# Two role adapters on one core: down features dealt in runs of eight, h kept in DRAM as the image the up phase loads

## The chip, the cores and the metric

The kernel runs on one core of a Trainium2 chip. Times are microseconds on the device, from start to end of an execution. A smaller time is better. A core has five engines with queues of their own: TensorE (PE, with its weight loads as PEld), VectorE (DVE), ScalarE (ACT), GpSimd (POOL) and SyncE (SP). SP only issues transfers here; ACT issues some as well, in the same queue as its arithmetic.

## The reference

Two layers are applied one after the other to 128 samples of 128 tokens with 1024 features, all in float32. A sample has one of three roles, and the role picks the weights. Cut to what matters, one layer is:

```python
# role: one of 0..2 for each of the 128 samples; x: [128, 128, 1024]
h = einsum("bsh,bhk->bsk", x, W_down[role]) + b_down[role]      # 1024 -> 512
h = gelu(h)
u = einsum("bsk,bkh->bsh", h, W_up[role]) + b_up[role]          # 512 -> 1024
y = x + u
x = (y - mean(y)) * rsqrt(var(y) + eps) * gamma[role] + beta[role]
```

The second layer does the same to the first one's result with its own weights.

## The kernel before

The samples are sorted by role on the chip, so that 63 pairs of equal role and two left-over samples make 64 items. There are four phases: down of layer 0, up of layer 0, down of layer 1, up of layer 1. Each phase runs over all 64 items with the weights of all three roles kept in SBUF (`wall`, eight slots of three roles). A pair is multiplied in the Winograd form of a 2x2 block product: seven products s1 to s7 instead of eight, with sums of blocks made beforehand (weights: T1 to T4 on VectorE; activations: `winograd_sums`, four subtractions or additions on POOL). A product is four (down) or two (up) blocks of 128 features that are summed in a PSUM bank.

**The layout.** TensorE wants features on the partitions. A tile `xq` (down) or `hq` (up) is loaded "quartered": quarter q of the features goes to partitions 32q to 32q+31, and partition 32q+t holds the tokens t, 32+t, 64+t and 96+t for that quarter. VectorE's transpose in blocks of 32 by 32 (L525 down, L584 up) then turns this into features on partitions, tokens along the row. In the down phase, element j*32 + i of a quarter ends on partition i of block j, so partition i works with the weight rows j*32 + i, which lie 32 rows apart in DRAM. Tokens come out in their own order.

**The way of h.** A down item writes its result into a tile `h` (two buffers, tokens on partitions). `Down.finish` (L559) stores it to the DRAM tile `hd[n]` from the ACT queue, in one transfer with rows of 2 KB. An up item loads it again with `Up.load` (L573), which calls `quartered`: eight transfers from SP of 64 KB each, in pieces of 512 bytes.

**The order.** All steps stand in a heap with due times, in units of a seventh of an item; they are emitted in the order of these times, and this is the order in which each engine's queue runs. Those of an item n that matter here, with 0 as the start of its first product: load of x at -11.9 (down) or of h at -11.5 (up); the rest of an up item's load, x for the residual, at -7 (L578); `prepare` with the transposes and POOL's sums at -8.8 (down) or -5.5 (up); products at 0, 2, ..., 12; the store of h at 12.5; in an up item the normalisation from 10.4 on and the store of its result from 13.5 (L651, to `mid` after layer 0 and to the output after layer 1). Since items start 7 units apart, two items' products alternate on TensorE, and the transposes of item n+2 stand in VectorE's queue ahead of the sums that end item n.

In a down pair, s1 and s3 and s5 and s7 add into one PSUM bank "b", s4 and s6 into a bank "e", s2 goes to a bank "a". Between two of them the bank's content is read: `begin` (L547, ACT) copies it to `h`, `end` (L551, VectorE) adds it to `h` and then L552 (ACT) applies gelu, `whole` (L555) applies gelu to the bank itself. So s3 waits for L547 after s1, and s7 waits for L551 after s5. L547 of item n+2 also waits until the store of `h` of item n has landed, as there are two buffers. In an up item the same places are L603 and L608 (VectorE, adding into the residual `x`).

**The weights.** The first down weights come straight into `wall` (`load_rows`, L147), four transfers of 256 KB for each half and role: role 0 at the start from ACT and SP, roles 1 and 2 later from SP. The weights of the three later phases are loaded one role at a time during the first phase (`Sums.load`, L203, four transfers of 512 KB), their blocks and sums are stored to DRAM (L212), and they come into `wall` slot by slot around each change of phase (L724). Before its first product TensorE works through a fixed row of products of zeros (L272).

Of the kernel before, what the change touches and what calls it, by code (L numbers as in the profile page):

```python
# [10 lines left out]
F32 = mybir.dt.float32  # L11
# [8 lines left out]
P = 128  # L20
SQ = 32
NQ = P // SQ
# [4 lines left out]
def kernel(  # L27
# [23 lines left out]

    nc = tc.nc
    B, S, H = x.shape
    R, _, K = layers[0][0].shape
# [11 lines left out]
    dram = ctx.enter_context(tc.tile_pool(name="mid", bufs=1, space=bass.MemoryType.DRAM))  # L68

    NI = NPAIR + 1  # L70
    hd = [dram.tile([2, S, K], F32, tag=f"hd{n}", name=f"hd{n}") for n in range(NI)]
    mid = [dram.tile([2, S, H], F32, tag=f"mid{n}", name=f"mid{n}") for n in range(NI)]
    scratch = {
        (layer, up): {
# [7 lines left out]
    def flat(tag, bufs, name, size=2048):  # L82
        return work.tile([P, size], F32, tag=tag, name=name, bufs=bufs)
# [5 lines left out]
    class Block:  # L89


        def __init__(self, slot):
            self.slot = slot
            self.v = wall[:, slot].rearrange("p (r n) -> p r n", n=W)
# [28 lines left out]
    def bias_table(v, which):  # L123

        n = v.shape[1] // 2
        t, load = table(v, which)

        def subtract(places=slice(0, R)):
            right, left = t[:, places, n:], t[:, places, 0:n]
            nc.vector.tensor_tensor(right, right, left, ALU.subtract)  # L130

        return t, load, subtract


    rows_of = [
        wall[:, 2 * k : 2 * k + 2]
        .rearrange("p k n -> p (k n)")
        .rearrange("p (r j h c) -> p r j h c", r=R, h=2, c=K // 2)
        for k in range(2)
    ]  # L140

    def load_rows(k, place, engine, kind):
        w = layers[0][0]
        role = reg(role_of, place, [kind], R - 1)
        for q in range(NQ):
            src = w[ds(role, 1), ds(q * H // NQ + k * P, P), :]
            engine.dma_start(  # L147
                rows_of[k][ts(q, SQ), place].rearrange("p j h c -> p j (h c)"),
                src.rearrange("o (j i) c -> i (o j) c", i=SQ),
            )  # L150

    first_weights = {
# [22 lines left out]
    class Sums:  # L175
# [2 lines left out]

        def __init__(self, layer, up, k):
            self.w = layers[layer][2 if up else 0]  # L180
            self.k = k
            n = self.w.shape[2] // 2
            room = tables[:, 0:2].rearrange("p t n -> p (t n)")
            self.whole = room[:, 0 : 4 * W].rearrange("p (m c) -> p m c", c=2 * n)
            block = lambda t: t.rearrange("p (j c) -> p j c", c=n)
            quarter = room[:, 0 : 4 * W].rearrange("p (k j h c) -> p k h j c", k=2, h=2, c=n)
            self.at = {
                "B11": quarter[:, 0, 0],
                "B12": quarter[:, 0, 1],
                "B21": quarter[:, 1, 0],  # L190
                "B22": quarter[:, 1, 1],
                "T1": block(room[:, 4 * W : 5 * W]),
                "T2": block(room[:, 5 * W : 6 * W]),
            }
            self.at["T3"], self.at["T4"] = self.at["B12"], self.at["B21"]
            self.to = {name: block(t[:, k]) for name, t in scratch[layer, up].items()}

        def load(self):
            role = reg(role_of, self.k, [ENG.SP], R - 1)
            rows = self.w.shape[1] // NQ  # L200
            for q in range(NQ):
                src = self.w[ds(role, 1), ds(q * rows, rows), :]
                nc.sync.dma_start(  # L203
                    self.whole[ts(q, SQ)], src.rearrange("o (m i) c -> i (o m) c", i=SQ)
                )

        def sum(self, name):
            a, b = {"T1": ("B12", "B11"), "T2": ("B22", "T1"), "T3": ("B22", "B12"), "T4": ("B21", "T2")}[name]
# [5 lines left out]
    class Phase:  # L214
# [4 lines left out]
        def load_bias(self, which):  # L219
            self.next_bias, load, self.subtract = bias_table(self.vectors[0], which)  # L220
            load()
# [108 lines left out]
    def gathered(name, values, where):  # L330

        ps = bank_a(name + "_ps")
        n = where.shape[1]
        nc.tensor.matmul(ps[0:SQ, 0:n], values, where, start=True, stop=True)
        t = const.tile([1, n], I32, name=name)
        nc.vector.tensor_copy(t, ps[0:1, 0:n])
        return t
# [17 lines left out]
    place = gathered("place", wide_place, onehot)  # L355
# [4 lines left out]
    def reg(t, s, engines, top):  # L360
        return nc.values_load(
            t[0:1, s : s + 1],
            engines=engines,
            min_val=0,
            max_val=top,
            skip_runtime_bounds_check_because="computed on the chip, always in this range",
        )

    def set_places(item, engines):

        n = item.n
        if n < NFIRST:
            item.places = [0, 0]
        elif n < NPAIR:
            item.places = [reg(place, 2 * n, engines, R - 1)] * 2
        else:
            item.places = [reg(place, 2 * n + s, engines, R - 1) for s in range(2)]
# [5 lines left out]
    def quartered(t, srcs):  # L383

        for s, src in enumerate(srcs):
            n = src.shape[-1] // NQ
            for q in range(NQ):
                nc.sync.dma_start(
                    t[s][ts(q, SQ)], src[:, ts(q, n)].rearrange("(a t) c -> t a c", t=SQ)
                )  # L390
# [6 lines left out]
    def winograd_sums(dst, a):  # L397


        half = a.shape[2] // 2  # L400
        a11, a12, a21, a22 = (a[:, i, ts(k, half)] for i in range(2) for k in range(2))
        nc.gpsimd.tensor_tensor(dst[:, 1], a11, a21, ALU.subtract)  # L402
        nc.gpsimd.tensor_tensor(a21, a21, a22, ALU.add)
        nc.gpsimd.tensor_tensor(dst[:, 0], a21, a11, ALU.subtract)  # L404
        nc.gpsimd.tensor_tensor(dst[:, 2], a12, dst[:, 0], ALU.subtract)
# [98 lines left out]
    class Down:  # L504
# [17 lines left out]
        def prepare(self):  # L522
            self.a = flat("t", 3, "xT" + self.tag).rearrange("p (s j c) -> p s j c", s=2, c=P)
            for s in range(2):
                nc.vector.transpose(  # L525
                    self.a[:, s].rearrange("p j (a t) -> p j a t", t=SQ),
                    self.xq[s].rearrange("p a (j i) -> p j a i", i=SQ),
                )
            self.sums = None
            if self.n < NPAIR:  # L530
                self.sums = flat("s", 3, "S" + self.tag, 1792)[:, 0:1536].rearrange(
                    "p (m j c) -> p m j c", m=3, c=P
                )
                winograd_sums(self.sums, self.a)
            set_places(self, [ENG.PE, ENG.Activation])
# [20 lines left out]

        def finish(self):
            at = 12.5
            return [(at, lambda: nc.scalar.dma_start(hd[self.n].rearrange("s p n -> p s n"), self.h))]  # L559

    class Up:
        LOAD, REST, PREPARE, SEED = -11.5, -7, -5.5, -4
# [4 lines left out]
            self.tag = f"u{layer}_{n}"  # L567

        def load(self):
            self.hq = flat("q", 4, "hq" + self.tag, H).rearrange(  # L570
                "p (s a c) -> p s a c", s=2, a=NQ
            )
            quartered([self.hq[:, s] for s in range(2)], [hd[self.n][s] for s in range(2)])  # L573

        def load_rest(self):
            self.x = flat("t", 3, "x" + self.tag).rearrange("p (s n) -> p s n", s=2)
# [93 lines left out]
    for k, ph in enumerate(phases):  # L670
        for m, n in enumerate(sequence):
            base = SLOTS * (k * NI + m)
            box = {}
            kind = Up if ph.up else Down

            def load(box=box, ph=ph, n=n, kind=kind, m=m):
                item = box["item"] = kind(ph, n)
                item.early = ph is phases[0] and m == 0
                if ph is phases[2] and m == 0:
                    item.SEED = -0.6  # L680
                if m == left_over_at + 1:
                    item.SEED = -1.5
                item.load()

            at(base + kind.LOAD, load)
            at(base + kind.REST, lambda box=box: box["item"].load_rest())

            def go(box=box, base=base):
                item = box["item"]
                item.prepare()  # L690
                for time, step in item.products() + item.finish():
                    at(base + time, step)


            prepare = {1: 3.5 - base, 2: 8.6 - base}.get(m, kind.PREPARE) if k == 0 else kind.PREPARE
            at(base + (-7.2 if ph is phases[2] and m < 3 else prepare), go)
# [43 lines left out]
    ph.bias, load_bias, subtract = bias_table(ph.vectors[0], 2)  # L740
    at(-12, lambda: load_bias([0]))
    at(-12, lambda: load_rows(0, 0, nc.scalar, ENG.Activation))
    at(-10, lambda: subtract(slice(0, 1)))
    at(-11, lambda: load_rows(1, 0, nc.sync, ENG.SP))
# [52 lines left out]
```

## Time and profile before

| | us |
|---|---|
| median of three runs | 3194.6 |
| lowest and highest run | 3193.32, 3203.36 |
| profiled execution | 3197.36 |
| its span, first to last instruction | 3195.3 |

Busy shares in stretches of 100 us of that execution (the stretches are named by their start):

| from, us | what runs | PE | DVE | ACT | POOL | DMA share |
|---|---|---|---|---|---|---|
| 100 | down, layer 0 | 95.9% | 42.0% | 25.2% | 46.8% | 0.74 |
| 800 | change to up, layer 0 | 94.7% | 54.3% | 37.3% | 46.2% | 0.82 |
| 1000 | up, layer 0 | 99.1% | 77.5% | 49.9% | 72.0% | 0.69 |
| 1600 | change to down, layer 1 | 90.8% | 46.2% | 33.9% | 56.7% | 0.89 |
| 1900 | down, layer 1 | 100.0% | 29.2% | 28.1% | 37.6% | 0.48 |

How to read it: a row of a group of instructions gives line, engine, operation, the tiles it writes and reads, the count, then the busy time, the mean in ns, and the idle time of the engine before these instructions with what ended it. A row of a timeline gives start and length in us, and in brackets the idle time before it and what ended that. A row of waits gives who waited for whom: total us, number of times, longest. A row of a DMA issue gives count, KB each, and the median time from issue to landing. "SPq" and "ACTq" are the queues that issue transfers. The clock that TensorE was granted was 0.994 of full speed over the span.

### The profile page before, as it was taken

What the parts mean: (1) busy time and instruction counts of PE and PEld (TensorE: products, weight loads), DVE (VectorE), ACT (ScalarE), POOL (GpSimd) and SP (SyncE); (2) the same over time, 40 slices, a digit from 0 to 9 for tenths busy, and PEclk for the clock granted to TensorE, in tenths of its full rate; (3) what the DMA queues carried; (4) which work ended last, traced back from release to release, by engine and by line L of the source; (5) the groups of instructions that cost most, each with busy time, mean ns of one, the idle gap of its engine ahead of it and who ended that gap; (6) DMA issues with size and microseconds to landing.
All of it is one profiled execution on the core that took longest, in us unless ns stands there. A gap on an engine that the chain in (4) does not pass through costs nothing. (4 is left out here: it accounts for less than half of the span.)

```text
span 3195.3 us, 43864 instructions
## 1 busy us (share of the span) xinstructions
PE 3131.9 (98%) x10824; PEld 2054.7 (64%) x10824; DVE 1772.8 (55%) x2783; ACT 1200.4 (38%) x2824; POOL 1791.7 (56%) x1399
## 2 busy tenths in 40 slices
PE   9999999999999999999989999999999999999997
PEld 6888888888534444444468888888884444444443
DVE  3533333334477777777743323233226777778877
ACT  1222222222345454545432222222224555454554
POOL 3544444444467776777754343443435777677775
PEclk9999999999999999999999999999999999999999
DMA  6776777777787666767796444544458766666664
GB/s 162 214 209 202 209 205 207 209 207 218 248 255 221 215 213 209 219 215 214 222 268 174 128 134 127 146 135 129 134 178 292 243 213 221 220 208 224 212 223 165
DMA packets 445506, 642.88 MB, mean 201 GB/s; under 512 B 46417, under 2 KB 316242, under 8 KB 445266
## 3 DMA queue, kind: packets, MB, share of 16 engines
q1 hardware_dynamic: 405986, 560.12, 59.6%
q10 hardware_dynamic: 39280, 79.96, 6.9%
q8 instruction: 102, 1.67, 0.2%
q14 instruction: 138, 1.13, 0.1%
HBM read 405.54 MB, written 234.36 MB: 200 GB/s over the span
## 5 line engine op out<-in xcount | busy, mean ns | idle before, releaser
L411 PE MATMUL bu<-wall,hTu 128*128 (+1 forms) x2048 | 929.9, 596 | 22.1 <-DVE xu L603 14.2
L411 PEld LDWEIGHTS bu<-wall,hTu 128*128 128x128 f32 x2048 | 386.3, 191 | 522.8 <-issue 426.2
L402 POOL TENSOR_TENSOR Sd<-xTd 128x512 f32<-128x512 f32 x126 | 168.6, 1338 | 842.0 <-DVE xTd L525 827.3
L632 POOL TENSOR_TENSOR varu<-varu,mhalf 128x1 f32<-128x1 f32 x256 | 334.8, 1308 | 414.6 <-ACT varu L631 367.0
L525 DVE STREAM_TRANSPOSE xTd<-xqd 128x1024 f32<-128x1024 f32 x256 | 307.9, 1230 | 438.8 <-PE bd L411 230.7
L411 PE MATMUL bd<-wall,xTd 128*128 (+1 forms) x2080 | 491.7, 380 | 7.8 <-DVE hd L551 5.2
L635 DVE SCALAR_TENSOR_TENSOR ou<-xu,meanu,tables 128x1024 f32<-128x1024 f32 x256 | 328.8, 1284 | 302.7 <-ACT ou L630 300.5
L411 PE MATMUL eu<-wall,hTu 128*128 (+1 forms) x1040 | 490.1, 594 | 4.1 <-DMA wall<-B 3.8
L411 PE MATMUL bd<-wall,Sd 128*128 (+1 forms) x2016 | 478.0, 380 | 4.4 <-ACT hd L547 4.4
L411 PEld LDWEIGHTS bd<-wall,xTd 128*128 128x128 f32 x2080 | 394.8, 190 | 66.2 <-DVE hd L551 7.3
L411 PEld LDWEIGHTS bd<-wall,Sd 128*128 128x128 f32 x2016 | 383.6, 190 | 59.4 <-POOL Sd L404 3.3
L411 PEld LDWEIGHTS eu<-wall,hTu 128*128 128x128 f32 x1040 | 198.0, 191 | 253.9 <-issue 240.6
L552 ACT ACTIVATE hd<-hd 128x256 f32<-128x256 f32 x382 | 157.2, 416 | 490.0 <-DVE hd L551 489.7
L626 ACT ACTIVATE partu<-statu 128x2 f32<-128x2 f32 x256 | 52.1, 203 | 759.4 <-DVE xu L608 759.4
L643 POOL TENSOR_TENSOR ou<-ou,tables 128x1024 f32<-128x1024 f32 x128 | 301.3, 2354 | 1.2 <-DMA hqu<-hd 0.9
L630 ACT ACTIVATE ou<-xu,meanu 128x1024 f32<-128x1024 f32 x256 | 294.0, 1148 | 19.1 <-DMA mid<-ou 4.2
L411 PE MATMUL ed<-wall,xTd 128*128 (+1 forms) x1072 | 252.9, 379 | 0.0
L402 POOL TENSOR_TENSOR hTu<-hTu 128x256 f32<-128x256 f32 x126 | 204.3, 1621 | 79.5 <-DVE hTu L584 77.7
L411 PE MATMUL ed<-wall,Sd 128*128 (+1 forms) x1008 | 238.1, 379 | 0.0
L411 PE MATMUL ad<-wall,xTd 128*128 (+1 forms) x1008 | 238.1, 379 | 0.0
L411 PE MATMUL au<-wall,hTu 128*128 (+1 forms) x504 | 236.8, 592 | 0.0
L411 PEld LDWEIGHTS ed<-wall,xTd 128*128 128x128 f32 x1072 | 203.7, 190 | 28.1 <-ACT ou L630 0.2
(96 smaller groups left out, 3348.6 us busy)
## 6 DMA issues: line engine op xcount, KB each, us to landing
xqd<-in_x_dram SPq DMA_DIRECT2D x512, 128.0 KB, 3.0
hd<-hd ACTq DMA_DIRECT2D x128, 512.0 KB, 2.8
hqu<-hd SPq DMA_DIRECT2D x1024, 64.0 KB, 4.1
xu<-in_x_dram SPq DMA_DIRECT2D x128, 512.0 KB, 5.3
mid<-ou SPq DMA_DIRECT2D x128, 512.0 KB, 5.2
xqd<-mid SPq DMA_DIRECT2D x512, 128.0 KB, 3.5
xu<-mid SPq DMA_DIRECT2D x128, 512.0 KB, 5.8
out_dram<-ou SPq DMA_DIRECT2D x128, 512.0 KB, 4.9
```

Source lines behind the costliest of these rows:

```text
L402: nc.gpsimd.tensor_tensor(dst[:, 1], a11, a21, ALU.subtract)
L411: nc.tensor.matmul(ps[:, 0:cols], a[:, j], w.rhs(r, j, cols), start=start and j == 0, stop=j == n - 1, skip_group_check=True,)
L525: nc.vector.transpose(self.a[:, s].rearrange("p j (a t) -> p j a t", t=SQ), self.xq[s].rearrange("p a (j i) -> p j a i", i=SQ),)
L552: nc.scalar.activation(y, y, AF.Gelu)
L626: nc.scalar.mul(part, self.stat[:, s], -1.0 / H)
L630: nc.scalar.activation(box["o"], self.x[:, s], AF.Square, bias=m, accum_out=v)
L632: nc.gpsimd.tensor_tensor(v, v, mhalf[:, 0:1], ALU.pow)
L635: nc.vector.scalar_tensor_tensor(box["o"], self.x[:, s], box["m"][:, 0:1], row(self.ph.gamma), ALU.add, ALU.mult)
L643: nc.gpsimd.tensor_tensor(o, o, row(self.ph.beta), ALU.add)
```

## The change

The order of the down features is changed. Feature i*8 + j of a quarter (8 of them in a row) now ends on partition i of block j, so a partition's eight weight rows of a quarter are neighbours in DRAM. The weight loads of the down phases follow: `load_rows` takes half of each partition's eight rows at a time, and `Sums.load` takes all eight as one run. The up weights stay as they were. The transposes of the down phase read the quarter with a step of eight elements, and write the tokens in the order (t a) in place of (a t), which is a step of four elements.

With that, the rows of `h` stand in the order of the image that an up item loads: partition p = 4t + a of `h` holds token 32a + t. The store of h writes each quarter of its columns to its own 128 x 128 block of a flat `hd[n]`, in pieces of 512 bytes. The up item then loads both samples with one transfer of 2 KB a partition and sample. Its transposes are unchanged, and the tokens come out in their own order again.

```diff
-    hd = [dram.tile([2, S, K], F32, tag=f"hd{n}", name=f"hd{n}") for n in range(NI)]
+    hd = [dram.tile([2, S * K], F32, tag=f"hd{n}", name=f"hd{n}") for n in range(NI)]
...
         for q in range(NQ):
-            src = w[ds(role, 1), ds(q * H // NQ + k * P, P), :]
+            src = w[ds(role, 1), ds(q * H // NQ, H // NQ), :]
+            src = src.rearrange("o (i m) c -> i (o m) c", i=SQ)
             engine.dma_start(
-                rows_of[k][ts(q, SQ), place].rearrange("p j h c -> p j (h c)"),
-                src.rearrange("o (j i) c -> i (o j) c", i=SQ),
+                rows_of[k][ts(q, SQ), place].rearrange("p j h c -> p j (h c)"), src[:, ts(k, NQ)]
             )
...
             self.w = layers[layer][2 if up else 0]
+            self.rows = "o (m i) c -> i (o m) c" if up else "o (i m) c -> i (o m) c"
...
                 src = self.w[ds(role, 1), ds(q * rows, rows), :]
-                nc.sync.dma_start(
-                    self.whole[ts(q, SQ)], src.rearrange("o (m i) c -> i (o m) c", i=SQ)
-                )
+                nc.sync.dma_start(self.whole[ts(q, SQ)], src.rearrange(self.rows, i=SQ))
...
                 nc.vector.transpose(
-                    self.a[:, s].rearrange("p j (a t) -> p j a t", t=SQ),
-                    self.xq[s].rearrange("p a (j i) -> p j a i", i=SQ),
+                    self.a[:, s].rearrange("p j (t a) -> p j a t", t=SQ),
+                    self.xq[s].rearrange("p a (i j) -> p j a i", i=SQ),
                 )
...
         def finish(self):
             at = 12.5
-            return [(at, lambda: nc.scalar.dma_start(hd[self.n].rearrange("s p n -> p s n"), self.h))]
+            dst = hd[self.n].rearrange("s (q p c) -> p (s q) c", q=NQ, p=P)
+            src = lambda: self.h.rearrange("p s (q c) -> p (s q) c", q=NQ)
+            return [(at, lambda: nc.scalar.dma_start(dst, src()))]
...
         def load(self):
-            self.hq = flat("q", 4, "hq" + self.tag, H).rearrange(
-                "p (s a c) -> p s a c", s=2, a=NQ
-            )
-            quartered([self.hq[:, s] for s in range(2)], [hd[self.n][s] for s in range(2)])
+            hq = flat("q", 4, "hq" + self.tag, H).rearrange("p (s n) -> p s n", s=2)
+            nc.sync.dma_start(hq, hd[self.n].rearrange("s (p n) -> p s n", p=P))
+            self.hq = hq.rearrange("p s (a c) -> p s a c", a=NQ)
```

## The prediction

> **What bounds the kernel now.** I read the page first (engines, groups, DMA issues), then the waits, then windows of 100 us, then timelines of the places where TensorE stops.
>
> ```profile
> span 3195.3 us, 43864 instructions
> PE 3131.9 (98%) x10824; PEld 2054.7 (64%) x10824; DVE 1772.8 (55%) x2783; ACT 1200.4 (38%) x2824; POOL 1791.7 (56%) x1399
> L525 DVE STREAM_TRANSPOSE xTd<-xqd 128x1024 f32<-128x1024 f32 x256 | 307.9, 1230 | 438.8 <-PE bd L411 230.7
> hd<-hd ACTq DMA_DIRECT2D x128, 512.0 KB, 2.8
> hqu<-hd SPq DMA_DIRECT2D x1024, 64.0 KB, 4.1
> ```
>
> TensorE is busy 98% of the span: 3195.3 - 3131.9 = 63.4 us are left, about 8 of them in the first 100 us and 19 in the last. No edit touches a matmul, so the change can only open, widen or close gaps. By windows of 100 us there is no gap from 1900 to 2000 (second down phase), 5.3 us from 800 to 900 (the first up phase begins) and 9.2 from 1600 to 1700 (the second down phase begins). Two gaps show the kinds, the first on TensorE, the second with VectorE's timeline:
>
> ```profile
> 827.37 1.88 PE L411 MATMUL au<-wall,hTu 128*128 128x512 f32 x4
> 833.02 3.75 PE L411 MATMUL eu<-wall,hTu 128*128 128x512 f32 x4 [3.77 <-DMA wall<-B]
> ```
> ```profile
> 81.78 1.99 PE L411 MATMUL bd<-wall,xTd 128*128 128x256 f32 x8 [1.13 <-DVE hd L551]
> ```
> ```profile
> 77.96 1.25 DVE L525 STREAM_TRANSPOSE xTd<-xqd 128x1024 f32<-128x1024 f32 x1 [10.66 <-DMA xqd<-in_x_dram]
> 80.17 1.25 DVE L525 STREAM_TRANSPOSE xTd<-xqd 128x1024 f32<-128x1024 f32 x1 [0.96 <-DMA xqd<-in_x_dram]
> 81.34 0.39 DVE L551 TENSOR_TENSOR hd<-bd,hd 128x256 f32<-128x256 f32 x1
> ```
>
> In the first, a weight block lands late, and the four matmuls after it take 3.75 us instead of 1.88. In the second, L551 (which frees the PSUM bank for s7) stands in VectorE's queue behind the transposes of a later pair, and those wait for x. Undisturbed, there is room:
>
> ```profile
> 1906.44 2.37 DVE L525 STREAM_TRANSPOSE xTd<-xqd 128x1024 f32<-128x1024 f32 x2 [3.09 <-PE bd L411]
> 1911.63 0.43 DVE L551 TENSOR_TENSOR hd<-bd,hd 128x256 f32<-128x256 f32 x1 [2.82 <-PE bd L411]
> ```
> ```profile
> 1916.54 1.89 PE L411 MATMUL bd<-wall,xTd 128*128 x8
> ```
>
> The two transposes end at 1908.81, L551 waits 2.82 us for its product, ends at 1912.06, and s7 takes the bank at 1916.54: 2.82 + 4.48 = 7.3 us to spare. Two waits carry the stores of h:
>
> ```profile
> ACT hd L547 <- DMA hd<-hd: 157.8, 55, 7.8
> ```
> ```profile
> SPq L388 <- DMA hd<-hd: 611.7, 95, 9.7
> ```
>
> The first is the reuse of the two h buffers. The second is a surprise: loads of x don't read hd. The issues' operands show eight completion semaphores (101, 105, 107 to 112) dealt round to all DMAs of SP and ACT; an issue waits until the DMA eight before it has landed, so SP's loads of x wait for ACT's store of h.
>
> [...]the store of h has 16 packets of 2 KB on each engine; alone they span 1.5 us (16 x 84 ns = 1.3), and 4.05 us at 250 us beside weight loads of 4 KB packets (16 x (84 + 159 ns) = 3.9). [...] here after the gap at 829 and that at 118 (2.4 us idle), and not after those of 1.7 and 2.1 us at 106 and 209.
>
> **The change, part by part.** The transposes of L525 now read with a step of 8 elements (32 bytes) and write with a step of 4 (16 bytes)[...]. The old price is 1230 ns for 1024 elements and 697 for 512 (L584), so 533 / 512 = 1.04 ns each[...]. Lower bound: no penalty, 1.23 us. Upper bound: read and write each cost a cycle more and don't overlap, 1.23 + 2 x 1.07 = 3.4. I take one cycle more, 2.30 us[...]. Undisturbed, a pair's two cost 2.1 us more against 7.3 to spare: nothing, and VectorE at 29% there can pay it. POOL's sums follow 2 us later, with s3 some 9 us off. It bites where L551 follows the transposes directly. Reading VectorE's timeline, that is at 81, 108, 135, 211, 284, 356, 503, 577, 649, 721, 795, 1635 and 1649 us; bank to spare before s7 is 0.06 us at five of them, under 0.6 at two, 0.8 to 2.7 at the rest. The first transpose often runs while the second half of x is still landing, so a pair costs 1.1 to 2.1 there: 7 x 1.3 = 9, 1 for the rest, 2 where the second down phase begins (L603 behind the transposes at 1603 us). The stalls at 106 and 209 (1.7 and 2.1 us) then pass the length after which the clock halved: 2 x 1.7 = 3. Sum **+15**; at no penalty 0; at the upper bound about 12 x 2.7 + 6 x 1.7 = 42.
>
> The store of h (L559, ACT queue) becomes 1024 packets of 512 bytes instead of 256 of 2 KB. 512-byte packets of the old loads take 30 ns: 64 x 30 = 1.9 us an engine instead of 1.4, so 0.4 to 0.6 later when alone. [...]with a 2 MB weight load queued (32 packets an engine) 1.9 + 32 x 0.159 = 7.0 instead of 3.9 us, +3. L547 has about 7.6 us from the issue until s3 needs the bank (1906.80 to 1914.4), and the landing's median is 2.8, the longest 8.5. But SP's next load of x waits for this landing, and in the 80 to 300 us stretch those loads are what the transposes wait for. I count 0.5 for seven late places and 1 more where the trace shows the store mixed with weights (96, 112, 199, 274 us): **+7**, bounds 2 and 20. ACT's own issue is 0.37 us now; four times the pieces may hold ACT for 1 us, beside its 28% nothing.
>
> The load of hd becomes one issue of 256 packets of 2 KB instead of eight. Packet time is 1024 x 30 = 31 us before, 256 x 100 = 26 after, over 16 engines: nothing. SP's queue gains: eight issues take 6.1 us of a pair's 12 in the up phase (5 DMAs a pair instead of 12, and the ring of eight semaphores stops holding them). Undisturbed, that hides. At 816 us the eight take 8.7 us, and the block that stalls TensorE is issued behind them, at 826. Sooner by 7 us it lands before 829: 3.8 of idle and 2.8 of half clock go, -6.6. The gaps from 880 to 940 (L603 late behind L584, which waits for hq) sum to 4.8. There the first quarter, issued at 865.3, lands at 875.1 with the last at 876.7: the bytes ahead set it, not the issues. I take half, -2.4. What is late next there is the store and load of `mid` and x. The gap of 7 us at 1600 (a late store of `mid`) and those of the left-over samples are untouched. Sum **-9**; bounds 0 and -17.
>
> Down weights: rows of 2 KB become runs of 8 KB (first layer) and 16 KB (second), 12 MB in all. 2 MB at the trace's 84 ns for 2 KB are 5.4 us, at 159 for 4 KB 5.1: -0.3 to -0.5 a load, **-1** in the two places (80, 106) where x waits behind them. At the start TensorE runs a fixed row of zero products until 28.7 us, so earlier weights gain nothing, and a slower second transpose (24.8 us) costs at most 0.5.
>
> Sum: +15 + 7 - 9 - 1 = +12 on the span of 3195.3 (the run took 3197.4, the median is 3194.6), so about **3206**.
>
> **Rivals.** *A, the forecast:* one more cycle an element, 3198 to 3216. *B, not slower:* the steps cost VectorE nothing[...]. For it: [...]L525 and L584 run at one element a cycle whatever else runs. Then +7 - 9 - 1 = -3, 3192; with the stores at their lower and the relief at its upper bound -16, 3179. It decides if L525 stays under about 1.5 us. *C, dearer steps:* L525 at 3.4 us gives +42 + 7 - 10 = +39, 3234[...]. *D, the stores alone:* at their upper bound (+20), without a dearer transpose, +10: 3205, as A but with L525 at 1.23. *E, no effect:* every piece hides, as in the second down phase; the near-zero room at seven places speaks against it.
>
> **Chances.** A 0.42, B 0.33, C 0.13, D 0.07, E 0.05. 0.3% (9.6 us) is about what a measurement of this kernel tells from no change. Slower by more: 0.6 of A, C, half of D = 0.42; faster by more: 0.75 of B with its tail = 0.25, and 0.02 of A; the rest, 0.31, is the same. The range reaches from B's upper part to C's lower: 3180 to 3228; A's own is 3198 to 3216.
>
> **What would show it.** L525's mean near 2.3 us, and L551 late behind it at more of the listed places (A); 1.2 (B, D); 3.4 (C). The gap at 829 gone and SP issuing `hqu` 128 times. `hd` landing at 3.3 us in the median, with more waits of L547. I am wrong if L525 stays at 1.2, or if TensorE stalls in the undisturbed second down phase.

## The result, and the profile after

The changed kernel takes 3191.9 us (median of 15 runs, 3189.2 to 3195.3). The kernel before, run beside it, takes 3200.2 us (15 runs, 3193.3 to 3204.9). The ratio is 0.9977, with a 95% interval of 0.9969 to 0.9984: faster by 0.23%, 7.4 us. The forecast was 3206, worked out as 12 us above a run of 3194 to 3197; against the 15 runs of before it would be 6 above. The profiled executions have spans of 3195.3 before and 3190.0 after.

Of the page of the changed kernel, the lines that answer to those shown of before. First the engines, then a row of a group and two rows of DMA issues:

```profile
span 3190.0 us, 41838 instructions
...
PE 3129.0 (98%) x10824; PEld 2055.3 (64%) x10824; DVE 1982.3 (62%) x2783; ACT 1199.2 (38%) x2824; POOL 1798.2 (56%) x1399
...
L527 DVE STREAM_TRANSPOSE xTd<-xqd 128x1024 f32<-128x1024 f32 x256 | 521.3, 2090 | 414.2 <-PE bd L413 216.9
...
hd<-hd ACTq DMA_DIRECT2D x128, 512.0 KB, 3.3
hqu<-hd SPq DMA_DIRECT2D x128, 512.0 KB, 6.9
```

(L525, L551 and L547 of before are L527, L553 and L549 here.) The transposes of the down phases take 2.09 us instead of 1.23, so VectorE works 213 us more over all of them. The loads of h are 128 instead of 1024, and the stores land in 3.3 us instead of 2.8. These parts came much as forecast (2.30 us for the transposes, 3.3 for the landing); the sign of the sum did not.

Where the time went shows in windows, before and then after. The columns are start and end, length, then busy us and count of each engine, the clock that TensorE was granted, the DMA share and GB/s:

```profile
300.00:800.00 500.00, 498.52 (x2308) 437.95 (x2307) 187.57 (x229) 132.25 (x370) 222.92 (x160) 1.00 0.73 209
800.00:1000.00 200.00, 191.26 (x475) 89.71 (x474) 128.90 (x222) 85.35 (x185) 115.94 (x99) 0.98 0.78 248
1000.00:1500.00 500.00, 495.82 (x1149) 216.89 (x1148) 385.02 (x655) 249.23 (x533) 353.64 (x283) 1.00 0.69 215
```
```profile
300.00:800.00 500.00, 495.93 (x2291) 434.20 (x2290) 252.95 (x225) 130.55 (x366) 221.78 (x158) 1.00 0.75 208
800.00:1000.00 200.00, 195.77 (x512) 95.99 (x511) 132.61 (x226) 87.42 (x192) 121.09 (x102) 1.00 0.75 258
1000.00:1500.00 500.00, 497.36 (x1154) 218.16 (x1153) 388.78 (x661) 252.72 (x538) 359.50 (x285) 1.00 0.64 216
```

The first number after the length is TensorE's busy time. It falls by 2.6 us in the first down phase (300 to 800) and rises by 4.5 at the start of the up phase and by 1.5 in its middle. From 800 to 1000 the clock also rises, from 0.98 to 1.00: no matmuls at half rate are left there.

Windows cut both executions at the same time, though TensorE is not at the same product then. Both run the same 10824 matmuls in the same order, so each one's start can be set against that of its counterpart:

| matmul that before starts at, us | 100 | 300 | 800 | 1000 | 1500 | 1700 | 2300 | end of the span |
|---|---|---|---|---|---|---|---|---|
| starts later in the changed kernel by, us | 2.2 | 4.1 | 10.1 | -0.1 | -2.4 | -1.2 | -1.0 | -5.3 |

So the first down phase loses 10 us, and the up phases gain more than that.

Two places show the two sides. First TensorE in the changed kernel, at the products that before stood around the gap at 829. Then SP's queue behind the load of h, before and after:

```profile
837.80 1.88 PE L413 MATMUL au<-wall,hTu 128*128 128x512 f32 x4
839.52 1.88 PE L413 MATMUL eu<-wall,hTu 128*128 128x512 f32 x4
```
```profile
815.95 8.67 SPq L388 DMA_DIRECT2D hqu<-hd  x8
826.04 0.34 SPq L724 DMA_DIRECT2D wall<-B  x1
```
```profile
826.38 0.62 SPq L575 DMA_DIRECT2D hqu<-hd  x1
828.54 0.32 SPq L727 DMA_DIRECT2D wall<-B  x1
```

No idle time stands in brackets, and the four matmuls of `eu` take 1.88 us, where before they took 3.75. The weight block follows 2.2 us after the load of h begins, instead of 10.1. By the clock it is issued 2.5 us later than before, but TensorE comes to these products 10.4 us later. This lateness alone does not close the gap: with seven tiny loads put back (below), TensorE is 13.3 us later here and the gap is there.

Then VectorE and TensorE in the first down phase:

```profile
204.55 2.09 DVE L527 STREAM_TRANSPOSE xTd<-xqd 128x1024 f32<-128x1024 f32 x1 [6.98 <-DMA xqd<-in_x_dram]
211.78 2.06 DVE L527 STREAM_TRANSPOSE xTd<-xqd 128x1024 f32<-128x1024 f32 x1 [5.14 <-DMA xqd<-in_x_dram]
213.74 0.38 DVE L553 TENSOR_TENSOR hd<-bd,hd 128x256 f32<-128x256 f32 x1
```
```profile
209.03 1.89 PE L413 MATMUL bd<-wall,Sd 128*128 128x256 f32 x8
214.18 1.99 PE L413 MATMUL bd<-wall,xTd 128*128 128x256 f32 x8 [3.26 <-DVE hd L553]
```

This is the stall that the forecast described: x lands late, the dearer transposes follow, L553 stands behind them, and TensorE waits for it. But only one of the two transposes counts, as the first one ends long before the second half of x is there.

### The profile page after: what moved, and what is told of

Its sections match the earlier page's. It is cut to its first block, busy times and chain, and to the rows that moved or that the text cites. A ratio compares the mean times of both kernels' runs of the same rounds, so it can differ in the third digit from the quotient of the medians.

```text
span 3190.0 us, 41838 instructions
## 1 busy us (share of the span) xinstructions
PE 3129.0 (98%) x10824; PEld 2055.3 (64%) x10824; DVE 1982.3 (62%) x2783; ACT 1199.2 (38%) x2824; POOL 1798.2 (56%) x1399
## 5 line engine op out<-in xcount | busy, mean ns | idle before, releaser
L413 PE MATMUL bu<-wall,hTu 128*128 (+1 forms) x2048 | 927.4, 595 | 14.4 <-DVE xu L606 8.8
L527 DVE STREAM_TRANSPOSE xTd<-xqd 128x1024 f32<-128x1024 f32 x256 | 521.3, 2090 | 414.2 <-PE bd L413 216.9
L413 PE MATMUL bd<-wall,xTd 128*128 (+1 forms) x2080 | 492.8, 380 | 17.2 <-DVE hd L553 14.2
L549 ACT COPY hd<-bd 128x256 f32<-128x256 f32 x256 | 95.2, 372 | 379.2 <-DMA hd<-hd 281.3
```

The lines of the kernel that those rows point to most:

```text
L413: nc.tensor.matmul(ps[:, 0:cols], a[:, j], w.rhs(r, j, cols), start=start and j == 0, stop=j == n - 1, skip_group_check=True,)
L527: nc.vector.transpose(self.a[:, s].rearrange("p j (t a) -> p j a t", t=SQ), self.xq[s].rearrange("p a (i j) -> p j a i", i=SQ),)
L549: nc.scalar.copy(self.part(s, k), ps[:, 0 : K // 2])
```

## The experiments

All ratios are against the kernel before, run on the same chip; 0.1% is 3.2 us. Where two kernels of different ratio are compared, the difference of the ratios is used and their intervals are added as squares.

### What each part costs

**Only the order of the down features** (the weight loads of the diff, and a transpose that only reads with a step):

```diff
-                    self.xq[s].rearrange("p a (j i) -> p j a i", i=SQ),
+                    self.xq[s].rearrange("p a (i j) -> p j a i", i=SQ),
```

> Only the order of the down features is changed: weight rows as runs, and the transposes of the down phases read with a step of 8 elements and write one run; store and load of h as before. Theory (dearer transposes cost some 9 us in the down phases, the single load of hd gives back some 14): if the reading step is what made L525 2.09 us, it is about 2.1 here too and the kernel is 5 to 9 us slower than before; if L525 stays at 1.23 it is the writing step, and the time is the same within 2 us. Rival (the gain comes from the longer runs of the weights): 5 us or more faster.

Ratio 1.0016 (1.0009 to 1.0022): 5.1 us slower. **Only the writing step**, with nothing that follows it (so the tokens of `h` stand in another order than the residual's):

```diff
-                    self.a[:, s].rearrange("p j (a t) -> p j a t", t=SQ),
+                    self.a[:, s].rearrange("p j (t a) -> p j a t", t=SQ),
```

> Before, with one thing changed: the transposes of the down phases write with a step of 4 elements. Nothing else follows it, so the tokens of h stand in another order than the residual's and the output is that of permuted tokens; no work is left out. Theory from the two partial kernels (each pays the dearer transpose once, and together they are 3 us dearer than the whole change): L525 at 2.0 us and the time 1 to 5 us above before. Rival (the transposes cost the +15 of the forecast, and something else gave 23 back): 12 us or more above.

Ratio 1.0015 (1.0007 to 1.0023): 4.8 us slower. The rows of the transposes, of the kernel with the reading step and of the kernel with the writing step:

```profile
L526 DVE STREAM_TRANSPOSE xTd<-xqd 128x1024 f32<-128x1024 f32 x256 | 507.7, 2015 | 407.3 <-PE bd L412 217.6
```
```profile
L525 DVE STREAM_TRANSPOSE xTd<-xqd 128x1024 f32<-128x1024 f32 x256 | 506.0, 2048 | 408.7 <-PE bd L411 235.4
```

Either step alone makes the transpose 2.0 us; both together make it 2.09. So the two don't add. The dearer transpose alone costs 4.8 us, not 15. As both kernels pay it once, the order of the weights is worth nothing that can be seen (5.1 - 4.8 = 0.3, with 3 us of uncertainty). **VectorE's time alone**, each transpose done twice on the old layout (work is doubled, the output is the same):

```diff
-                nc.vector.transpose(
...
+                for again in range(2):
+                    nc.vector.transpose(
...
```

> Before, with every transpose of the down phases done twice, the same output written again: VectorE spends 2.46 us where it spent 1.23, a little more than the 2.09 of the changed kernel, and no DMA differs. Theory (VectorE's time is what costs in the first down phase): 8 to 14 us slower than before, the loss in the first 800 us. Rival (the small packets of the stores of h made the loss there): within 3 us of before.

Ratio 1.0045 (1.0029 to 1.0061): 14 us slower with 1.23 us more for each transpose, where 0.82 more cost 4.8. It fits a price that rises faster than the time added, as it comes from what passes the slack. The rival that VectorE's time costs nothing falls. That the loss lies in the first 800 us did not come out: counted as in the table further down, its profiled execution has 27.2 us of stalls there, 4 more than before, while 6 more stand from 1500 to 1700 (20.6).

**The store alone**: h in DRAM in blocks of 128 x 128, still loaded by eight transfers.

```diff
...
+            dst = hd[self.n].rearrange("s (q p c) -> p (s q) c", q=NQ, p=P)
...
+            blocks = hd[self.n].rearrange("s (q a t c) -> s q t a c", q=NQ, a=NQ, t=SQ)
+            for s in range(2):
+                for q in range(NQ):
+                    nc.sync.dma_start(self.hq[ts(q, SQ), s], blocks[s, q])
...
```

> Before, with h kept in DRAM by blocks of 128 x 128: the store writes 1024 pieces of 512 bytes as in the changed kernel, and the load is still eight transfers with pieces of 512 bytes, now out of those blocks. Transposes and weights as before. Theory (relief is in the load alone, small stores cost a little): 0 to 4 us slower. Rival 1, the forecast's term: +7. Rival 2 (the store itself is what gained): 5 us or more faster.

Ratio 1.0027 (1.0016 to 1.0038): 8.6 us slower. The forecast's +7 stands, and my later theory of 0 to 4 falls. **Only the way of h** (writing step, image, one load; weights as before):

> Only the way of h is changed: the transposes of the down phases write with a step of 4 elements and read as before, h is stored as the image and loaded with one transfer; weights as before. Theory: the gap at 829 is gone, the time is 5 to 14 us below before, nearer to 14 if L525 stays at 1.23 here and nearer to 5 if it is at 2.1. Rival (weights): the same as before or slower, as the gain is not in this part.

Ratio 0.9970 (0.9963 to 0.9977): 9.6 us faster, though L525 is at 2.04 us. The whole gain of the change is in this part, and since transposes (+4.8) and store (+8.6) are in it, what the load gives back would be over 20 us by this sum; measured directly it is less, as the next part shows.

### What the single load gives

**The changed kernel with eight loads of the same image**, pieces of 2 KB:

```diff
...
-            nc.sync.dma_start(hq, hd[self.n].rearrange("s (p n) -> p s n", p=P))
...
+            for s in range(2):
+                for q in range(NQ):
+                    nc.sync.dma_start(self.hq[ts(q, SQ), s], image[s, q])
```

> The changed kernel, but the image of h is loaded in eight transfers of 64 KB a pair (sample by sample, quarter of the partitions by quarter) in place of one; pieces of 2 KB as in the changed kernel. Theory (the single issue made the relief): the gap near 829 is back and most of the relief is lost, 3195 to 3206, that is up to 6 us above before. Rival (the pieces of 2 KB made it): within 3 us of the changed kernel, 7 us below before.

Ratio 1.0028 (1.0015 to 1.0041): 9.0 us above before, somewhat more than the theory allowed, and 0.51% above the changed kernel, 16 us (11 to 21). **The single load, and seven tiny ones behind it**:

```diff
             nc.sync.dma_start(hq, hd[self.n].rearrange("s (p n) -> p s n", p=P))
+            for i in range(7):
+                small_load = idle.tile([SQ, 16], F32, tag="idle", name=f"idle{self.tag}_{i}")
+                nc.sync.dma_start(
+                    small_load, hd[self.n][0].rearrange("(p n) -> p n", p=P)[0:SQ, 0:16]
+                )
```

> The changed kernel, with seven tiny loads (32 rows of 64 bytes, used by nobody) added from SP behind the single load of h of each pair: the number of issues is that of the kernel before, the bytes are not. Theory (issues and places in the ring of eight semaphores are what the single load saves): 10 to 16 us above the changed kernel, with the gap near 829 back. Rival (how the bytes are cut into transfers): within 3 us of the changed kernel.

Ratio 1.0032 (1.0021 to 1.0043): 0.55% above the changed kernel, 18 us (13 to 22), for loads that move 14 KB a pair. So putting the issues back takes the relief away with eight loads of 64 KB (16 us) as with seven of 2 KB (18 us). An issue takes time in SP's queue (0.43 us in the median for a load of h in the kernel before) and one of the eight completion semaphores; the runs don't separate the two. In the trace of the kernel before, 2033 of the 2902 issues wait on the semaphore that they count on themselves, and 51 loads of x start 0.02 us (median) after a store of h on the same semaphore has landed. SP's queue in the kernel with the tiny loads, and TensorE:

```profile
829.24 1.00 SPq L575 DMA_DIRECT2D hqu<-hd  x1
830.29 8.19 SPq L578 DMA_DIRECT2D idleu<-hd  x7
839.58 0.34 SPq L732 DMA_DIRECT2D wall<-B  x1
```
```profile
840.66 1.88 PE L413 MATMUL au<-wall,hTu 128*128 128x512 f32 x4
847.03 3.75 PE L413 MATMUL eu<-wall,hTu 128*128 128x512 f32 x4 [4.50 <-DMA wall<-B]
```

Seven loads of 2 KB hold SP's queue for 8.19 us. Behind them stands the weight block, and TensorE waits 4.50 us for it and then runs at half rate: the gap of the kernel before, made again. The waits of SP from 1000 to 1500 us (who waited, for whom, total us, times, longest) show why, in the order before, changed kernel, seven tiny loads:

```profile
SPq L651 <- POOL ou L643: 121.5, 41, 6.3
SPq L388 <- DMA mid<-ou: 42.4, 40, 2.2
SPq L388 <- DMA xu<-in_x_dram: 24.3, 38, 1.3
```
```profile
SPq L654 <- POOL ou L646: 354.3, 41, 10.0
```
```profile
SPq L659 <- POOL ou L651: 77.3, 41, 5.0
SPq L659 <- DMA hqu<-hd: 44.7, 40, 2.5
SPq L578 <- DMA mid<-ou: 40.9, 42, 2.2
SPq L578 <- DMA xu<-in_x_dram: 24.9, 39, 1.3
```

The wait for POOL (for the result that is to be stored) is what SP has to spare. It is 24% of the stretch before, 71% after and 15% with the tiny loads. The waits of load instructions for DMAs that have nothing to do with them are for these semaphores: in the kernel before, each of the 78 (66.7 us) is at an issue whose one wait is on its own semaphore. In the changed kernel, with five DMAs an item, there is none in this stretch. **Between one and eight**:

```diff
...
+            for s in range(2):
+                nc.sync.dma_start(hq[:, s], hd[self.n][s].rearrange("(p n) -> p n", p=P))
...
```

> The changed kernel with the image of h loaded in two transfers of 256 KB a pair, one for each sample. The kernel with eight loads of the same image was 16 us above the changed kernel. Theory (each issue more costs SP's queue and a place in the ring): about 2 us above the changed kernel, 5 below before. Rival (what counts is that the first sample is complete early; a pair's one transfer gives both late): faster than the changed kernel by 2 us or more.

> The changed kernel with the image of h loaded in four transfers of 128 KB a pair (sample by sample, two halves of the partitions). An up item then has 8 DMAs, as many as there are semaphores in the ring; 5 with one load, 12 with eight. Theory of the ring (nothing until an item has more than eight): within 3 us of the changed kernel. Rival (each issue costs SP the same): 5 to 8 us above it.

Two loads: 0.9970 (0.9958 to 0.9982), 2 us below the changed kernel, within the uncertainty of 4.5; which of the two theories holds isn't settled. Four (two halves of the partitions for each sample): 0.9989 (0.9982 to 0.9995), 4 us above it, uncertain by 3; here too neither theory is settled. The costs are about nothing for two, 4 for four and 16 for eight. A fixed sum for each further issue (16.3 / 7 = 2.3 us) would give 2.3 and 7, at the edge of the two intervals, so it is unlikely but not excluded. With four, SP no longer waits for foreign DMAs between 1000 and 1500 us, and its spare time is 245 us.

**Four loads in the kernel before**, one for each quarter of the features, both samples in each:

```diff
...
+            rows = hd[self.n].rearrange("s p n -> (s p) n")
+            for q in range(NQ):
+                nc.sync.dma_start(
+                    hq[ts(q, SQ)].rearrange("p (b c) -> p b c", c=P),
+                    rows[:, ts(q, P)].rearrange("(b t) c -> t b c", t=SQ),
+                )
...
```

> Before, with the load of h in four transfers of 128 KB a pair in place of eight of 64 KB; pieces of 512 bytes, store, transposes and weights as before. Theory (the number of issues in SP's queue is what counted): at least half of the relief, 5 to 10 us faster than before, since nothing else is dearer. Rival (pieces of 2 KB or the order of the image made the gain): no change within 2 us.

Ratio 1.0077 (1.0061 to 1.0092): 25 us slower, against both expectations. The waits of the up transposes for their load, in the kernel before and in this one:

```profile
DVE hTu L584 <- DMA hqu<-hd: 21.2, 41, 3.9
```
```profile
DVE hTu L588 <- DMA hqu<-hd: 62.3, 73, 2.4
```

Cut this way, no sample is complete before the last of the four lands, and VectorE, which was 77% busy in the up phase before, waits for it with everything behind it. By the count of the table further down the loss lies in the up phases: 13 us more of stalls from 1000 to 1500 and 10 more after 2300. The four loads sample by sample lost nothing like this. That the cut by quarters is the cause was not tried by itself (those loads also had larger pieces). **Contiguous transposes and the image all the same**: the store puts the tokens in order, in four transfers from ACT.

```diff
...
+            dst = hd[self.n].rearrange("s (q t a c) -> a t (s q) c", q=NQ, t=SQ, a=NQ)
...
+                for a in range(NQ):
+                    nc.scalar.dma_start(dst[a], src[ts(a, SQ)])
...
```

> Before, with its contiguous transposes of 1.23 us and its weights, but with the image of h in DRAM and the single load: the tokens' order is made by the store, in four transfers a pair, one for each run of 32 partitions, from ACT. Theory: the relief without the dearer transposes, 10 to 14 us below before and 3 to 5 below the changed kernel; less where three more issues on ACT (about 0.4 us each) or three more places in the ring of semaphores cost something. Rival (ACT's queue is the price, as L547 and gelu stand behind the issues): at or above before.

Ratio 1.0057 (1.0044 to 1.0070): 18 us slower, with transposes of 1.23 us. SP's and ACT's queues, and then VectorE, in the first down phase:

```profile
585.47 8.24 SPq L388 DMA_DIRECT2D xqd<-in_x_dram  x14
```
```profile
581.71 1.86 ACTq L564 DMA_DIRECT2D hd<-hd  x4
```
```profile
589.80 1.25 DVE L525 STREAM_TRANSPOSE xTd<-xqd 128x1024 f32<-128x1024 f32 x1 [11.53 <-DMA xqd<-in_x_dram]
591.95 1.25 DVE L525 STREAM_TRANSPOSE xTd<-xqd 128x1024 f32<-128x1024 f32 x1 [0.90 <-DMA xqd<-in_x_dram]
593.12 0.39 DVE L551 TENSOR_TENSOR hd<-bd,hd 128x256 f32<-128x256 f32 x1
```

ACT issues the four stores from 581.71 to 583.57, SP's next loads of x begin at 585.47, and the transposes wait 11.53 us for x. From 300 to 780 us VectorE waits 170.6 us for x (43 times), in the kernel before 92.3 (32 times). SP's loads of x wait 107.3 us for stores of h (29 times; 133.7 and 26 before) and 44.2 for other loads (43 times; 11.3 and 3 before). That the three more stores take semaphores for which SP's loads of x then wait is my reading of this; no run tried it by itself. Counted as in the table further down, the stalls up to 800 us are 42.6 us instead of 22.9, which is all of the loss. The rival (at or above before) was right in the number; its mechanism, ACT's own time (1.86 us for the four issues), isn't what this timeline shows, though no run tried that by itself either.

### What the place of the transposes costs

The transposes of all down items, 2.9 units later, behind the L551 of s5 (items 1 and 2 of the first phase and the first three of the second have due times of their own and keep them):

```diff
-        LOAD, REST, PREPARE, SEED = -11.9, -11.8, -8.8, -4
+        LOAD, REST, PREPARE, SEED = -11.9, -11.8, -5.9, -4
```

> Before, with the transposes and POOL's sums of a down item placed 2.9 units (about 5 us) later in the queues, behind the L551 of the product s5 that used to follow them; no work changes. Theory (L551 behind transposes that wait for x makes the stalls of the first down phase): the stalls at 81, 106, 209 and 284 us shrink or go, 3 to 8 us faster than before. Rival (the stalls come from x and weights that land late, whatever the order): same within 2 us, or slower, as s1 then waits for the transposes.

> The changed kernel with the transposes of a down item placed 2.9 units later, behind the L551 of s5. Theory: the price of the dearer transposes goes with their place ahead of L551, so that the gain is larger than in the kernel before with the same shift: 8 to 14 us below the changed kernel, 3176 to 3184. Rival: as the transposes take 4.2 us a pair and s1 now has 5 us less room, no gain or a loss.

> The same shift, with only the way of h changed and the order of the weights as before. Theory: within 3 us of the changed kernel with the shift, as the order of the weights is worth nothing; and the fastest of all if it is a little in the weights' disfavour. Rival: 5 us or more from it.

Before with the shift 1.0022 (1.0013 to 1.0032), 7 us slower; the changed kernel with it 0.9976 (0.9968 to 0.9985), and with the old weights 0.9976 (0.9966 to 0.9985). The first two theories fall, the third stands. The traces show where it goes: in the changed kernel the stalls between 100 and 800 us shrink from 18 to 9.5 us with the shift, but those of the first 100 us, where the first products now wait for their transposes, grow from 13 to 22. So the shift was made for items 3 to 61 of a phase only:

```diff
+            if kind is Down and 3 <= m < NPAIR - 1:
+                prepare = -5.9
```

> The changed kernel with the transposes of the down items 3 to 61 of a phase placed 2.9 units later, and those of the first three and the last two items where they were. Theory: what the shift of all items lost in the first 100 us and around 2360 us (some 10 and 4 us of stalls) is not lost, and what it gained between 200 and 800 us (about 7) stays: 5 to 10 us below the changed kernel. Rival: the loss at the two ends was not of the shift, same within 2 us.

> Before, with the shift of the middle items as in the version of the changed kernel that was 10.6 us below it. Theory (a part of that gain is the price of the dearer transposes, some 5 us, which a shift takes away): the gain here is smaller, 3 to 7 us below before. Rival (the shift is worth the same in both, so it has nothing to do with the transposes' price): 9 to 12 us below before.

> The changed kernel with the shift of the middle items and with the image of h loaded in two transfers, one for each sample. Theory (two loads are as good as one): within 3 us of the same kernel with one load, 3178 to 3184. Rival (the earlier first sample helps): 3 us or more below it.

The changed kernel with it: 0.9944 (0.9931 to 0.9958), median 3181.3 us, the fastest version here, 10.6 us below the changed kernel. With two loads as well: 0.9949 (0.9934 to 0.9964), no better. The kernel before with the shift: 0.9987 (0.9979 to 0.9996), 4 us. The shift is worth 6 us more where the transposes are dear, uncertain by 6; by the time at which the matmul of 800 us starts, it gives 11.5 us in the changed kernel and 4.0 in the kernel before. VectorE at the stall of 210 us, in the fastest version:

```profile
203.35 0.42 DVE L552 TENSOR_TENSOR hd<-bd,hd 128x256 f32<-128x256 f32 x1 [7.11 <-PE bd L412]
203.69 2.09 DVE L526 STREAM_TRANSPOSE xTd<-xqd 128x1024 f32<-128x1024 f32 x1
208.05 2.09 DVE L526 STREAM_TRANSPOSE xTd<-xqd 128x1024 f32<-128x1024 f32 x1 [2.26 <-DMA xqd<-in_x_dram]
```

L552 has gone ahead, and TensorE has no idle time there.

### The stalls of all these kernels side by side

Time from one matmul's start to the next, less a pace of 0.2156 us down and 0.427 us up, added up by stretch of the profiled execution. The commonest steps in the traces before and after are 0.216 and 0.429 us, so of each row's third column some 3 us and of its sixth some 5 are pace. The rest is idle time and time at half rate; the first column also holds the start, 9 to 11 us in each. The totals differ as the spans do (75.0 - 69.7 = 3195.3 - 3190.0):

| kernel | loads of h | 0-800 | 800-1000 | 1000-1500 | 1500-1700 | 1700-2300 | 2300-end | all |
|---|---|---|---|---|---|---|---|---|
| before | 8 | 22.9 | 14.7 | 10.2 | 14.3 | 0.6 | 12.4 | 75.0 |
| reading step, weights | 8 | 24.3 | 13.0 | 10.2 | 16.4 | 0.6 | 11.3 | 75.8 |
| writing step | 8 | 22.8 | 12.7 | 10.3 | 18.7 | 0.6 | 14.1 | 79.3 |
| store in blocks | 8 | 25.1 | 12.1 | 9.8 | 16.8 | 0.6 | 17.2 | 81.6 |
| changed, eight loads | 8 | 31.7 | 12.6 | 9.4 | 15.9 | 0.9 | 15.4 | 86.0 |
| changed, seven tiny | 1+7 | 33.8 | 16.7 | 8.2 | 16.3 | 0.9 | 12.9 | 88.8 |
| changed, four loads | 4 | 33.8 | 5.4 | 6.9 | 17.1 | 0.9 | 9.1 | 73.2 |
| changed, two loads | 2 | 31.8 | 2.2 | 6.2 | 15.4 | 0.9 | 10.1 | 66.7 |
| before, shift of 3 to 61 | 8 | 18.9 | 13.9 | 9.5 | 15.4 | 0.6 | 17.0 | 75.3 |
| **changed** | 1 | 30.7 | 6.8 | 7.9 | 15.5 | 0.9 | 8.0 | 69.7 |
| way of h alone | 1 | 29.9 | 4.6 | 7.5 | 15.3 | 0.7 | 10.6 | 68.7 |
| changed, shift of 3 to 61 | 1 | 21.4 | 2.2 | 6.8 | 14.4 | 0.6 | 9.9 | 55.3 |

Single executions scatter, so groups are to be read. The six kernels with eight issues and no shift have 13.6 us on average from 800 to 1000, 9.7 from 1000 to 1500 and 13.9 from 2300 on. The three with one load and no shift or two loads (changed, way of h alone, two loads) have 4.5, 7.2 and 9.6. So the single load gives 9 + 2.5 + 4.3, some 16 us. In the first column, the transposes alone or the store alone change nothing beyond 2.2 us; both together cost 7 to 11. With the shift the changed kernel is 2.5 above the kernel before with the same shift. These stretches are cut by time, so a late kernel carries a stall over an edge; counted matmul by matmul, both together cost 8.5 to 12.3 up to 800, and the gain from 800 to 1000 is 10 instead of 9.

## Why the prediction was wrong

The forecast was rival A, slower at 3206. Its mechanism is there, yet the time is that of rival B (3192), whose mechanism is not: L525 did not stay under 1.5 us. That the time met B's number is chance. (A "cycle" in the forecast is the 1.04 ns that an element took in the kernel before. The gaps that it names at 829 and 118 us are those after which TensorE ran at half rate: granted clock 0.5 from 831.5 and from 121.5 us.)

The step that failed is the one from dearer transposes and stores to stalls of TensorE; the relief by the load was mis-sized the other way. Up to 800 us the forecast had some +19 (13 for the transposes, 7 for the store, -1 for the weights), and the profiled executions differ by +10.1. Behind that it had -9 from 800 to 1000, measured -10.2, and +2 where the second down phase begins, measured +1.2. It had nothing for 1000 to 1500 and for the time after 2300, where -2.3 and -4.3 were measured. The runs say the same: all parts but the single load cost 9.0 us together (5 to 13, the changed kernel with eight loads), where the forecast had 15 + 7 - 1 = 21, and the single load then gives 16, where it had 9. By the terms of the sum:

- **L525, +15 (bounds 0 and 42).** The duration was about right (2.09 us, forecast 2.30), though the one cycle more was a guess that nothing measured stood behind. The step that turned it into a cost failed: alone it costs 4.8 us (2 to 7). "7 x 1.3 = 9" was 3.3 with the writing step alone: the idle times at 81, 106, 135, 209, 284, 577 and 721 us grew by 0.2 to 0.7 each. Against that the one at 118 shrank by 1.1, and the half rate behind it (1.7 us) did not come, so nothing is lost up to 800 in that execution. It is 4.3 us longer in all: 4.4 come from 1500 to 1700, and 1.8 lost after 2300 stand against 2.0 gained from 800 to 1000. The timeline at 204 us shows why each place costs so little: the first transpose is hidden, so a pair costs at most 0.8, and its part in any slack less. The 3 us of half clock did not come in the changed kernel: TensorE idled 3.26 us at 210 and went on at full rate, as the eight matmuls in 1.99 us show.
- **Store, +7 (bounds 2 and 20).** The size was right, 8.6 us; the place was not, so the number is in part luck. The forecast counted it at late loads of x in the first 300 us. The 3 us more beside a weight load were an estimate; what the traces show is a landing of 3.3 us in the median and 11.5 at the longest, instead of 2.8 and 8.5. In the profiled execution of the store alone, 6.7 us longer than before, nothing is lost there; 2.5 us come from 300 to 800, 2.5 from 1500 to 1700 and 4.9 after 2300, less what is gained between. What the sum did not have is that up to 800 us store and transposes make each other dearer (the first column). That later x and a dearer transpose hit the same L551 would explain it; no run tried that by itself. Over the whole kernel no such surplus shows: 9.0 us for both, where the parts sum to 13.7, uncertain by 6.
- **Load, -9 (bounds 0 and -17).** Mis-sized: 16 to 18 us by the two kernels that put the issues back. The -9 was about right for the places it looked at: the gap at 829 is gone, and the stalls from 880 to 940, counted as in the table, went from 7.2 us to 2.8. What it left out are 1000 to 1500 us and everything after 2300, which it called untouched or hidden. "Undisturbed, that hides" failed: SP's spare time there was 24% and not more, which fits that a late piece behind eight issues is slow to catch up. How the 16 us split beyond the stretches of the table isn't resolved.
- **Weights, -1.** Nothing that can be measured, 0.3 with 3 us of uncertainty.

Measured one by one, 4.8 + 8.6 + 0.3 - 16.3 = -2.6; the change gave -7.4 (-9.9 to -5.1). The uncertainty is as large as the rest of about 5. The larger pieces of the load may be in it; that stays open.

The count of `hqu`, the landing of `hd` and the further waits of L547 (281 us in 115 waits, from 158 in 55) came as written. Neither of the signs that the forecast named for being wrong showed: L525 rose, and the second down phase did not stall more. That phase kept its 0.6 to 0.9 us of stalls: there the spare 7.3 us hid the dearer transposes, about half of the 213 us more, as forecast.

## What to carry to other kernels

A queue that issues transfers is an engine with a load of its own: count its issues for each item and look at its spare time (here the wait for the thing it is to store) before you judge that fewer issues would gain nothing. Here the eight issues of one load took 8.67 us at 816 us, and that wait rose from 24% to 71% of the up phase's middle when seven of them went. The dearer transposes (0.8 us each) cost what passed the slack at the few places where something stood behind them, and of two in a row that wait for two transfers only the last one counted. Moving them behind the instruction they block gave 10.6 us where only the middle of a phase was moved and nothing where all of it was; alone they cost 4.8. The loads by quarters suggest, though no run shows it by itself, to cut loads by what the first consumer needs and not by layout alone.

## What was not expected of the hardware

- The transposes took 2.015 us with a reading step of 32 bytes, 2.048 with a writing step of 16 bytes and 2.09 with both, against 1.23. That is 0.77 to 0.84 ns more an element, about as much for a step on one side as for both. No other step was tried, and what sets this price was not shown.
- The length of a stop did not settle whether half rate followed. In the kernel before, a stop of 2.43 us at 118 was followed by it (granted clock 0.5 for 3.4 us); in the changed kernel one of 3.26 us at 210 was not (granted clock 1.00 from 214 to 218); and with the seven tiny loads a shorter one of 2.82 us at the same place was (0.62 from 214 to 218). The forecast's 3 us for half rate took it from the length of two stops; with these three, such a term is better written as a chance than as a threshold.
- Seven loads of 2 KB took 8.19 us in SP's queue at 830 us, about as long as the eight of 64 KB at 816 us in the kernel before (8.67 us).
